# A scan layer and a spectral layer on one core: the scan layer's first and last steps get other banks, another load order and interleaved norm halves

## The chip, the core and the metric

The kernel runs on one core of a Trainium2 chip. A core has five engines with instruction queues of their own: TensorE (PE, matrix products into PSUM), VectorE (DVE), ScalarE (ACT), GpSimd (POOL) and SyncE (SP), which here issues the transfers between the chip's memory and the on-chip memory SBUF. An engine works through its queue in order, and waits on semaphores for the other engines and for transfers. PSUM has eight banks, each of 512 fp32 values on 128 partitions.

The metric is the device time of one execution in microseconds (us), as the median of several runs. Fewer is better.

## The reference

Two layers run one after the other on `x` of shape (4, 128, 128, 128): batch, channels, rows, columns. All is fp32.

```python
# layer 0: a selective scan over the 64 tokens of every 8 x 8 window
tn = layernorm(t) * ln_g + ln_b                 # over the 128 channels
xi, z = split(tn @ W_in + b_in)                 # 256 channels each
xc = silu(causal_conv(xi, conv_w, K=4) + conv_b)
dr, Bm, Cm = split(xc @ W_x)                    # 8, 16 and 16 channels
delta = softplus(dr @ dt_w + dt_b)
h = exp(delta * A) * h + (delta * xc) * Bm      # scan over 64 tokens, 16 states
y = (sum(h * Cm) + xc * D) * silu(z)
x = x + y @ W_out + b_out
# layer 1: norm over channels, 2-D FFT, spectral filters, inverse FFT, MLP, residual
zn = layernorm(x) * gamma + beta
Uf = rfft2(zn) * conj(Phi)                      # 16 filters
S = einsum('bdlxy,lhd->bhxy', irfft2(Uf), Theta)
out = x + W2(gelu(W1(S) + b1)) + b2
```

## The kernel before

Four stages follow each other: `mamba_layer` (layer 0, and the norm of layer 1), `spectra`, `mix` and `images_and_mlp` (the rest of layer 1). Only `mamba_layer` is concerned here.

**Rows and steps.** The image is cut into 64 "rows" (4 images, 16 strips of 8 pixel rows): 1024 tokens of 128 channels each, tile `xt`. A row's scans are cut into 32 units, each of 128 partitions (8 channels x 16 states) and 2x512 tokens. The kernel is written out as one list of slots `s`. Unit `s` is scanned in slot `s` (`scan`, L401): VectorE multiplies the replicated `delta*x` by B (L408) and runs the scan (L410), then POOL multiplies by C (L418). Slots 0 to 2047 hold the scans of all 64 rows.

**What lies around the scans.** Row r's preparation begins some 30 slots before its scans, so from the second row on it stands between the scans of the row before. Row 0's preparation has slots -35 to -6, with no scans beside it. In the same way the last row's output stands, in part, behind the last scan. The order within every engine's queue is the order in which the Python code emits the instructions (`manual_schedule`): in each slot first the `takes`, then fetches, replication, decay, then `make`, `took`, the scan, and `lates`.

The steps of one row's preparation, with their lines: load of `xt` (L173); the norm in two halves of 512 tokens, each of `ln_center` (L150, four matmuls that subtract the mean), `ln_scale` (L157 to L162, ACT: squares with accumulation, Ln, Exp, scaled copies), `ln_back` (L168, four matmuls that turn the tokens back) and `f_affine` (L180, into `tn`); four groups `f_conv` (L202, L200) and four `f_in` (L188), each emptied by ACT (L207, L193); Silu on ACT (L210, L211); for two channel halves the matmuls of `f_dt` (L227) and `f_bc` (L217), ACT's Abs, Relu, Exp and Ln (L237 to L242), and POOL's sum and product (L245, L251), whose results `delta` and `du` SP stores to memory (L254, L257). From there SP fetches them again, replicated over the states, as `dr` (L342, for `exp(delta*A)` at L391) and, for seven of 32 units, `ur` (L352). For the other units TensorE replicates `du` into a bank pair (L376).

The steps behind the scans: `b_gate` (L263), `b_out` and its bias (L272, L274, L280) in two halves into `x1t`, the store of `x1t` (L283), the second norm (same helpers, `b_affine` at L288 into `z`) and the store of `z` (L291). `spectra` loads `z` from memory again (L491).

**PSUM.** The eight banks are given out as: three pairs `du` (the replicated units), one bank `y` (the sums over states) and one bank `one`, which all preparation and output steps share:

```python
        def one(name):
            return ps.tile([P, HB], F32, tag="one", name=name)
```

**Before the first slot** SP loads 17 constants (L61). VectorE and TensorE then fold the causal convolution into the input product (L84 to L106, with matmuls L93 into `one`), and two small weights into one (L108 to L116). `fold` and `fold2` are one after the other in the buffer `ab`. VectorE clears four `dA` tiles and `tn` (L121, L125). Row 0's `xt` is loaded by its `take` in slot -35, which stands behind all of this in SP's queue.

Of the kernel before, what the change touches and what calls it, by code (L numbers as in the profile page):

```python
# [13 lines left out]
F32 = mybir.dt.float32  # L14
BF16 = mybir.dt.bfloat16
AF = mybir.ActivationFunctionType
# [3 lines left out]
P = 128  # L20
# [5 lines left out]
DR = 8  # L26
W = 128
HB = 512
# [5 lines left out]
def mamba_layer(tc, d, x, x1, zb, deltas, dus):  # L34
# [8 lines left out]
    nc = tc.nc  # L43
    B = x.shape[0]
    NH, NW = W // WS, W // WS
    n = WS * W
    U = 32
# [5 lines left out]
    with ExitStack() as ctx:  # L53
# [2 lines left out]
        sb = ctx.enter_context(tc.tile_pool(name="l0_sb", bufs=1))  # L56
        ps = ctx.enter_context(tc.tile_pool(name="l0_ps", bufs=1, space=PSUM))

        def load(name):
            t = cp.tile(list(d[name].shape), F32, tag=name, name=f"c_{name}")  # L60
            nc.sync.dma_start(t, d[name])  # L61
            return t

        def half(t, h):
# [5 lines left out]
        nc.vector.memset(eps, EPS)  # L70
        zeros = cp.tile([P, 2, WS], F32, tag="zeros", name="zeros")
        nc.vector.memset(zeros, 0.0)
        names = "center rsel ssel ln_g ln_b W_in b_in conv_w conv_b W_bc dt_b A_log D W_out b_out gamma beta"
        c = {k: load(k) for k in names.split()}
        A = cp.tile([P, 32], F32, tag="A", name="A")
        nc.scalar.activation(A, c["A_log"], AF.Exp)
        nc.vector.tensor_scalar(A, A, -1.0, None, ALU.mult)
# [6 lines left out]
        fold = sb.tile([P, n], F32, tag="ab", name="fold")  # L84
        nc.sync.dma_start(fold[:, : 2 * P], d["W_in_t"])
# [23 lines left out]
        fold = sb.tile([P, n], F32, tag="ab", name="fold2")  # L109
        nc.sync.dma_start(fold[:DR, : 2 * P], d["W_xdt"])  # L110
        nc.sync.dma_start(fold[:DR, HB : HB + 2 * P], d["dt_w"])
        for ch in range(2):
            t = ps.tile([P, HB], F32, tag="one", name="p_fold")
            w = fold[:DR, ch * P : (ch + 1) * P]
            nc.tensor.matmul(t[:, : 2 * P], w, fold[:DR, HB : HB + 2 * P], start=True, stop=True)
            nc.vector.tensor_copy(W_dt[:, ch], t[:, : 2 * P])  # L116
# [12 lines left out]

        rs = [SimpleNamespace(py={}, yz={}) for _ in rows_all]  # L130
        takes, lates, makes = {}, {}, {}

        def take(slot, f):
            takes.setdefault(slot, []).append(f)
# [8 lines left out]


        def ln_center(o, src, h):
            o.ln = one("ln_cen")
            for q in range(HB // P):
                at = h * HB + q * P
                tokens = getattr(o, src)[:, at : at + P]
                nc.tensor.matmul(o.ln[:, q * P : (q + 1) * P], tokens, c["center"], start=True, stop=True)  # L150

        def ln_scale(o):
            o.cs = sb.tile([P, HB], F32, tag="cs", name="cs", bufs=2)
            r = sb.tile([P, HB // P], F32, tag="ln_r", name="ln_r", bufs=2)
            blocks = [slice(q * P, (q + 1) * P) for q in range(HB // P)]
            for q, k in enumerate(blocks):
                nc.scalar.activation(o.cs[:, k], o.ln[:, k], AF.Square, accum_out=r[:, q : q + 1])  # L157

            nc.scalar.activation(r, r, AF.Ln, bias=eps, scale=1.0 / P)
            nc.scalar.activation(r, r, AF.Exp, scale=-0.5)  # L160
            for q, k in enumerate(blocks):
                nc.scalar.activation(o.cs[:, k], o.ln[:, k], AF.Copy, scale=r[:, q : q + 1])  # L162

        def ln_back(o):
            o.lb = one("ln_back")
            for q in range(HB // P):
                k = slice(q * P, (q + 1) * P)
                nc.tensor.matmul(o.lb[:, k], o.cs[:, k], ident, start=True, stop=True)  # L168


        def f_load(o, b, rows):
            o.xt = sb.tile([P, n], F32, tag="xt", name="xt", bufs=3)
            nc.sync.dma_start(o.xt, x[b, :, rows, :].rearrange("c i w -> c (i w)"))  # L173

        def f_affine(o, h):

# [113 lines left out]
        def b_store_z(o, b, rows):  # L290
            nc.sync.dma_start(zb[b][:, rows, :].rearrange("c i w -> c (i w)"), o.z)  # L291

        def norm(o, src, affine, at):
            for h in range(2):
                made(at + 2 * h, partial(ln_center, o, src, h), partial(ln_scale, o))
                made(at + 2 * h + 1, partial(ln_back, o), partial(affine, o, h))

        for r, (o, (b, rows)) in enumerate(zip(rs, rows_all)):  # L300
            s = U * r - LEAD
            for h in range(2):
                for k in range(2):
                    late(s + LEAD + 16 * h + 8 * k + 11, partial(b_gate, o, h, k))
                made(s + (61, 67)[h], partial(b_out, o, h), partial(b_out_bias, o, h))
            take(s + 72, partial(b_store, o, b, rows))
            norm(o, "x1t", b_affine, s + 89)
            take(s + 96, partial(b_store_z, o, b, rows))
        for r, (o, (b, rows)) in enumerate(zip(rs, rows_all)):
            s = U * r - LEAD  # L310
            take(s - 5, partial(f_load, o, b, rows))
            norm(o, "xt", f_affine, s - 1)
            for i in range(4):
                m, h = divmod(i, 2)
                made(s + (5, 7, 10, 12)[i], partial(f_conv, o, m, h), partial(f_conv_out, o, m, h))
                made(s + (8, 9, 13, 14)[i], partial(f_in, o, 2 + m, h), partial(f_in_z, o, 2 + m, h))
                made(s + (17, 18, 21, 22)[i], partial(f_dt, o, m, h), partial(f_dt_out, o, m, h))
                made(s + (19, 20, 23, 24)[i], partial(f_bc, o, h, m), partial(f_bc_out, o, h, m))
            take(s + 15, partial(f_silu, o))
            for k in range(2):  # L320
                take(s + 19 + 4 * k, partial(f_soft, o, k))
                take(s + 19 + 4 * k, partial(f_delta, o, k))
                take(s + 21 + 4 * k, partial(f_store, o, r, k))
                take(s + 21 + 4 * k, partial(f_du, o, k))
                take(s + 24 + 4 * k, partial(f_store_du, o, r, k))
# [473 lines left out]
```

## Time and profile before

| | us |
|---|---|
| median of 3 runs | 10449.41 |
| lowest and highest | 10445.54, 10451.61 |
| the profiled execution | 10450.79 |
| its span, first to last instruction | 10448.8 |
| first unit's product (L408) begins | 104.69 |
| last scan (L410) ends | 7158.44 |
| `z` of the last row is stored (L291) | 7185.69 |
| first matmul of `spectra` | 7195.28 |

The profile is of one execution, so its times add up to 10448.8 us, not to the median. Of the span, VectorE is busy 86%, TensorE 89%, GpSimd 79%, ScalarE 62%. These are means over stages with different limits. In the scan phase VectorE is busy 936 to 940 of every 1000 us and POOL about 904 to 911 (stretches from 1400 to 2400 and from 3400 to 4400 us). The constants that are loaded first are small: each of the large ones (`rsel`, `W_in`, `W_bc`) has 256 KB and lands 2.6 to 2.9 us after its issue; a row of `x` has 512 KB. TensorE's busy share must be read with care: matmuls are pipelined, and the same matmul takes about twice as long when the granted clock is low.

### The profile page before, as it was taken

Reading aid. Unit: us, or ns where it says so; the run is one execution under the profiler, and the core shown is the slowest. Engines: PE = TensorE matmul, PEld = TensorE weight load, DVE = VectorE, ACT = ScalarE, POOL = GpSimd, SP = SyncE. Lnnn points to the kernel's source line nnn. Section 1 sums busy time; section 2 is a strip of 40 time slices with the busy share of each in tenths; the row PEclk is TensorE's granted clock in tenths of the full one; section 3 lists DMA queues with packets and bytes.
Section 4 is the critical chain, followed back from the end, with each engine's and each line's share of the span. In section 5 each row is a group of like instructions: output and inputs, shape, how many; then the busy total and the mean of one; then the engine's idle time right before and its main releaser. Section 6 shows DMA issues by size and latency. Waiting matters only on the chain.

```text
span 10448.8 us, 143616 instructions
## 1 busy us (share of the span) xinstructions
PE 9293.9 (89%) x48900; PEld 5027.3 (48%) x48900; DVE 8980.1 (86%) x7234; ACT 6524.3 (62%) x12463; POOL 8231.4 (79%) x4188
## 2 busy tenths in 40 slices
PE   6888888888888888888888888887889999998999
PEld 2333333333333333333333333335889999998766
DVE  5999999999999999999999999995389999998433
ACT  5776777777777777777777677773344444444433
POOL 5899998998998998989989899893079999997000
PEclk8999989989999999999999999997999999999999
DMA  4777677777776776777767767775521111112332
GB/s 150 213 229 220 213 223 218 217 219 219 225 221 213 226 222 214 223 217 225 221 210 228 218 215 223 219 221 160 148 68 34 35 35 36 36 36 62 136 128 93
DMA packets 1168110, 1794.06 MB, mean 172 GB/s; under 512 B 368641, under 2 KB 436497, under 8 KB 1166225
## 3 DMA queue, kind: packets, MB, share of 16 engines
q1 hardware_dynamic: 1167376, 1784.88, 56.6%
q8 instruction: 387, 6.34, 0.3%
q14 instruction: 347, 2.83, 0.1%
HBM read 1481.44 MB, written 303.04 MB: 171 GB/s over the span
## 4 chain that ended last, share of the span: by engine, by line
PE 58%; ACT 20%; DVE 9%; DMA 7%; issue 4%; POOL 1%; SPq 1%; DVEq 0%; ACTq 0%; POOLq 0%
PE p_v L578 13%; DVE hs L410 6%; PE p_du L376 6%; PE p_conv L202 5%; DMA dr<-delta 5%; ACT part L589 5%; PE p_bc L217 5%; PE p_dt L227 4%; PE p_y L428 4%; DVE p_du L408 3%; PE p_out L274 2%; ACT dA L391 2%; PE ln_cen L150 2%; ACT p_du L391 2%; PE p_h L672 2%
## 5 line engine op out<-in xcount | busy, mean ns | idle before, releaser
L418 POOL TENSOR_TENSOR hs<-hs,bc 128x1024 f32<-128x1024 f32 x2048 | 4806.3, 2372 | 408.9 <-DVE hs L410 357.3
L410 DVE TENSOR_TENSOR_SCAN hs<-dA,p_du 128x1024 f32<-128x1024 f32 x1600 | 3659.0, 2287 | 208.2 <-DVE p_du L408 4.9
L591 POOL TENSOR_TENSOR acc<-acc,part 128x512 f32<-128x512 f32 x1430 | 1829.3, 1319 | 640.6 <-ACT part L589 640.6
L408 DVE TENSOR_TENSOR p_du<-p_du,bc 128x1024 f32<-128x1024 f32 x1600 | 1935.8, 1210 | 219.6 <-PE p_du L376 215.0
L391 ACT ACTIVATE dA<-dr,A 128x504 f32<-128x504 f32 x3200 | 2072.0, 704 | 33.1 <-DVE hs L410 23.7
L578 PE MATMUL p_v<-theta,xk 128*128 128x128 f32 x16640 | 1941.4, 277 | 87.9 <-ACT part L589 51.9
L578 PEld LDWEIGHTS p_v<-theta,xk 128*128 128x128 f32 x16640 | 1883.1, 192 | 146.2 <-ACT part L589 118.9
L595 DVE SCALAR_TENSOR_TENSOR acc<-p_v,phi,acc 128x512 f32<-128x512 f32 x2470 | 1672.4, 740 | 114.2 <-PE p_v L578 87.5
L376 PE MATMUL p_du<-du,c_rsel 32*128 32x512 f32 x6400 | 1364.3, 678 | 370.2 <-DVE hs L410 370.2
L589 ACT ACTIVATE part<-p_v,phi 128x512 f32<-128x512 f32 x1430 | 904.8, 686 | 803.9 <-PE p_v L578 800.3
L428 PE MATMUL p_y<-hs,c_ssel 128*32 128x512 f32 x8192 | 1225.7, 634 | 134.2 <-DVE yz L263 82.9
L410 DVE TENSOR_TENSOR_SCAN hs<-p_du,ur 128x1024 f32<-128x1024 f32 x448 | 1019.0, 2275 | 86.8 <-ACT p_du L391 60.5
L356 POOL TENSOR_TENSOR ur<-ur,bc 128x1024 f32<-128x1024 f32 x448 | 1063.1, 2373 | 10.7 <-DMA ur<-du 10.7
L202 PE MATMUL p_conv<-tn,W_conv 128*128 128x512 f32 x2048 | 1007.3, 616 | 3.2 <-ACT xc L207 1.6
L376 PEld LDWEIGHTS p_du<-du,c_rsel 32*128 32x128 f32 x6400 | 370.4, 192 | 1081.1 <-issue 780.6
L227 PE MATMUL p_dt<-xc,W_dt 128*128 128x512 f32 x1024 | 619.8, 736 | 48.0 <-ACT dl L238 42.3
L391 ACT ACTIVATE p_du<-dr,A 128x504 f32<-128x504 f32 x896 | 613.9, 685 | 29.1
L428 PEld LDWEIGHTS p_y<-hs,c_ssel 128*32 128x32 f32 x8192 | 184.3, 111 | 887.5 <-issue 571.2
L207 ACT ACTIVATE xc<-p_conv,b_conv 128x512 f32<-128x512 f32 x256 | 176.2, 688 | 639.3 <-PE p_conv L202 639.3
L245 POOL TENSOR_TENSOR dl<-dl,ab 128x1024 f32<-128x1024 f32 x128 | 302.6, 2364 | 338.5 <-ACT ab L242 338.5
L202 PEld LDWEIGHTS p_conv<-tn,W_conv 128*128 128x128 f32 x2048 | 346.8, 189 | 455.2 <-issue 247.9
L168 PE MATMUL ln_back<-ident,cs 128*128 128x128 f32 x2048 | 339.5, 316 | 222.3 <-ACT cs L162 216.6
(100 smaller groups left out, 10341.0 us busy)
## 6 DMA issues: line engine op xcount, KB each, us to landing
dr<-delta SPq DMA_DIRECT2D x4096, 256.0 KB, 5.2
ur<-du SPq DMA_DIRECT2D x896, 256.0 KB, 6.4
delta<-dl SPq DMA_DIRECT2D x128, 512.0 KB, 2.9
du<-du SPq DMA_DIRECT2D x128, 512.0 KB, 5.4
xf<-x SPq DMA_DIRECT2D x8, 4160.0 KB, 16.4
xk<-xf SPq DMA_DIRECT2D x130, 256.0 KB, 3.8
sf<-acc SPq DMA_DIRECT2D x520, 64.0 KB, 1.7
s<-sf SPq DMA_DIRECT2D x8, 4160.0 KB, 13.4
```

The source lines that it names most:

```text
L202: nc.tensor.matmul(windows(o.pc), W_conv[:, ch, k], moved, start=(k == 0), stop=(k == K - 1))
L356: nc.gpsimd.tensor_tensor(fetched[s], fetched[s], both(o.bc[0], h), ALU.mult)
L376: nc.tensor.matmul(u.bank[:, j % 2], c["rsel"][p, u.i], half(u.o.du[p, u.ch], u.h), start=True, stop=True)
L391: nc.scalar.activation(u.dA[:, q, :, 1:], u.delta[:, q].rearrange("p (w t) -> p w t", t=L)[:, :, 1:], AF.Exp, scale=A[:, g : g + 1],)
L408: nc.vector.tensor_tensor(u.bu, u.bu, both(u.o.bc[0], u.h), ALU.mult)
L410: nc.vector.tensor_tensor_scan(u.hs.rearrange("p q t -> p (q t)"), u.dA.rearrange("p q w t -> p (q w t)"), u.bu.rearrange("p q t -> p (q t)"),
L418: nc.gpsimd.tensor_tensor(u.hs, u.hs, both(u.o.bc[1], u.h), ALU.mult)
L428: nc.tensor.matmul(o.py[h, ch][32 * j : 32 * j + 32], c["ssel"][:, u.i], units[s + j // 2].hs[:, j % 2], start=(u.i == 0), stop=False, ski ...
L578: nc.tensor.matmul(t[:, b], o.xk[:, b, r], theta[:, k], start=True, stop=True)
L589: nc.scalar.activation(part, v[of], AF.Copy, scale=factor)
L591: nc.gpsimd.tensor_tensor(apart, apart, part, ALU.add)
L595: nc.vector.scalar_tensor_tensor(mine, v[of], factor, mine, ALU.mult, ALU.add)
```

## The change

Six edits, all in `mamba_layer`:

1. ACT's table set with Ln, Exp and others is loaded first of all, by name.
2. Row 0's tokens are loaded first on SP's queue, ahead of the constants. ACT issues four transfers itself: `W_in_t`, `conv_w`, `b_in`, `conv_b`. The other constants come in another order.
3. `fold2` gets a buffer of its own (one of the two `z` buffers), so its two loads need not wait for `fold`.
4. The fold matmuls, and every step that calls `one` in a slot before -1 or from 2048 on, use the three bank pairs `du` in turn (the first bank of a pair) instead of the bank `one`. At that time the units don't use them.
5. Row 0's first norm and the last row's second norm emit center, center, back, back instead of center, back, center, back. The last row's norm follows its output directly, and its `z` store stands right behind its `x1t` store. The other rows keep their order.
6. The `dA` tiles and `tn` are cleared by POOL instead of VectorE.

```diff
+        nc.scalar.preload_act_table_set("natural_log_exp_and_others")
+
         def load(name):
             t = cp.tile(list(d[name].shape), F32, tag=name, name=f"c_{name}")
-            nc.sync.dma_start(t, d[name])
+            (nc.scalar if name in "conv_w b_in conv_b" else nc.sync).dma_start(t, d[name])
+            return t
+
+        def load_tokens(b, rows):
+            t = sb.tile([P, n], F32, tag="xt", name="xt", bufs=3)
+            nc.sync.dma_start(t, x[b, :, rows, :].rearrange("c i w -> c (i w)"))
             return t
...
-        names = "center rsel ssel ln_g ln_b W_in b_in conv_w conv_b W_bc dt_b A_log D W_out b_out gamma beta"
+
+        fold = sb.tile([P, n], F32, tag="ab", name="fold")
+        fold2 = sb.tile([P, n], F32, tag="z", name="fold2", bufs=2)
+        nc.scalar.dma_start(fold[:, : 2 * P], d["W_in_t"])
+        first = load_tokens(*rows_all[0])
+        names = "center ln_g ln_b conv_w b_in conv_b W_in D A_log dt_b W_bc rsel ssel W_out b_out gamma beta"
         c = {k: load(k) for k in names.split()}
+        nc.sync.dma_start(fold2[:DR, : 2 * P], d["W_xdt"])
+        nc.sync.dma_start(fold2[:DR, HB : HB + 2 * P], d["dt_w"])
...
-            t = ps.tile([P, HB], F32, tag="one", name="p_fold")
+            t = ps.tile([P, 2, HB], F32, tag="du", name="p_du", bufs=3)[:, 0]
...
-            nc.vector.memset(t, 0.0)
+            nc.gpsimd.memset(t, 0.0)
             dAs.append(t)
...
-        nc.vector.memset(tn, 0.0)
+        nc.gpsimd.memset(tn, 0.0)

         def one(name):
+
+            if one.free:
+                return ps.tile([P, 2, HB], F32, tag="du", name="p_du", bufs=3)[:, 0]
             return ps.tile([P, HB], F32, tag="one", name=name)
...
-        def norm(o, src, affine, at):
+        def norm(o, src, affine, *slots):
             for h in range(2):
-                made(at + 2 * h, partial(ln_center, o, src, h), partial(ln_scale, o))
-                made(at + 2 * h + 1, partial(ln_back, o), partial(affine, o, h))
+                made(slots[h], partial(ln_center, o, src, h), partial(ln_scale, o, h))
+                made(slots[2 + h], partial(ln_back, o, h), partial(affine, o, h))
...
+            last = r == R - 1
             take(s + 72, partial(b_store, o, b, rows))
-            norm(o, "x1t", b_affine, s + 89)
-            take(s + 96, partial(b_store_z, o, b, rows))
+            norm(o, "x1t", b_affine, *((s + k) for k in ((68, 69, 70, 71) if last else (89, 91, 90, 92))))
+            take(s + (72 if last else 96), partial(b_store_z, o, b, rows))
...
-            take(s - 5, partial(f_load, o, b, rows))
-            norm(o, "xt", f_affine, s - 1)
+            if r == 0:
+                o.xt = first
+            else:
+                take(s - 5, partial(f_load, o, b, rows))
+            norm(o, "xt", f_affine, *((s + k) for k in ((-1, 0, 1, 2) if r == 0 else (-1, 1, 0, 2))))
...
         for s in range(-LEAD - 5, U * R + 99 - LEAD):
+            one.free = not -1 <= s < U * R
```

`ln_center`, `ln_scale` and `ln_back` take the half `h` as well and keep `o.ln[h]` and `o.cs[h]` apart, so that both halves can be under way; `cs` had two buffers already.

More of the change, by code (lines that the diff above doesn't have):

```diff
@@ L83, in mamba_layer @@
         early = cp.tile([P, 2, WS, K - 1], F32, tag="early", name="early")
-        fold = sb.tile([P, n], F32, tag="ab", name="fold")
-        nc.sync.dma_start(fold[:, : 2 * P], d["W_in_t"])
         for ch in range(2):
             nc.vector.tensor_scalar(skip[:, ch], ident, c["D"][:, ch : ch + 1], None, ALU.mult)
-            t = ps.tile([P, HB], F32, tag="one", name="p_fold")
+            t = ps.tile([P, 2, HB], F32, tag="du", name="p_du", bufs=3)[:, 0]
             for k in range(K):
@@ L108, in mamba_layer @@
         W_dt = cp.tile([P, 2, 2 * P], F32, tag="W_dt", name="W_dt")
-        fold = sb.tile([P, n], F32, tag="ab", name="fold2")
-        nc.sync.dma_start(fold[:DR, : 2 * P], d["W_xdt"])
-        nc.sync.dma_start(fold[:DR, HB : HB + 2 * P], d["dt_w"])
         for ch in range(2):
-            t = ps.tile([P, HB], F32, tag="one", name="p_fold")
-            w = fold[:DR, ch * P : (ch + 1) * P]
-            nc.tensor.matmul(t[:, : 2 * P], w, fold[:DR, HB : HB + 2 * P], start=True, stop=True)
+            t = ps.tile([P, 2, HB], F32, tag="du", name="p_du", bufs=3)[:, 0]
+            w = fold2[:DR, ch * P : (ch + 1) * P]
+            nc.tensor.matmul(t[:, : 2 * P], w, fold2[:DR, HB : HB + 2 * P], start=True, stop=True)
             nc.vector.tensor_copy(W_dt[:, ch], t[:, : 2 * P])
@@ L120, in mamba_layer @@
             t = cp.tile([P, 2, WS, L], F32, tag=f"dA{i}", name="dA")
-            nc.vector.memset(t, 0.0)
+            nc.gpsimd.memset(t, 0.0)
             dAs.append(t)
         tn = cp.tile([P, NW, K - 1 + L], F32, tag="tn", name="tn")
-        nc.vector.memset(tn, 0.0)
+        nc.gpsimd.memset(tn, 0.0)
         def one(name):
+            if one.free:
+                return ps.tile([P, 2, HB], F32, tag="du", name="p_du", bufs=3)[:, 0]
             return ps.tile([P, HB], F32, tag="one", name=name)
-        rs = [SimpleNamespace(py={}, yz={}) for _ in rows_all]
+        rs = [SimpleNamespace(py={}, yz={}, ln={}, cs={}) for _ in rows_all]
         takes, lates, makes = {}, {}, {}
@@ L145, in ln_center @@
         def ln_center(o, src, h):
-            o.ln = one("ln_cen")
+            o.ln[h] = one("ln_cen")
             for q in range(HB // P):
@@ L149, in ln_center, with ln_scale @@
                 tokens = getattr(o, src)[:, at : at + P]
-                nc.tensor.matmul(o.ln[:, q * P : (q + 1) * P], tokens, c["center"], start=True, stop=True)
-        def ln_scale(o):
-            o.cs = sb.tile([P, HB], F32, tag="cs", name="cs", bufs=2)
+                nc.tensor.matmul(o.ln[h][:, q * P : (q + 1) * P], tokens, c["center"], start=True, stop=True)
+        def ln_scale(o, h):
+            cs = o.cs[h] = sb.tile([P, HB], F32, tag="cs", name="cs", bufs=2)
             r = sb.tile([P, HB // P], F32, tag="ln_r", name="ln_r", bufs=2)
@@ L156, in ln_scale @@
             for q, k in enumerate(blocks):
-                nc.scalar.activation(o.cs[:, k], o.ln[:, k], AF.Square, accum_out=r[:, q : q + 1])
+                nc.scalar.activation(cs[:, k], o.ln[h][:, k], AF.Square, accum_out=r[:, q : q + 1])
             nc.scalar.activation(r, r, AF.Ln, bias=eps, scale=1.0 / P)
@@ L161, in ln_scale, with ln_back @@
             for q, k in enumerate(blocks):
-                nc.scalar.activation(o.cs[:, k], o.ln[:, k], AF.Copy, scale=r[:, q : q + 1])
-        def ln_back(o):
+                nc.scalar.activation(cs[:, k], o.ln[h][:, k], AF.Copy, scale=r[:, q : q + 1])
+        def ln_back(o, h):
             o.lb = one("ln_back")
@@ L167, in ln_back @@
                 k = slice(q * P, (q + 1) * P)
-                nc.tensor.matmul(o.lb[:, k], o.cs[:, k], ident, start=True, stop=True)
+                nc.tensor.matmul(o.lb[:, k], o.cs[h][:, k], ident, start=True, stop=True)
         def f_load(o, b, rows):
-            o.xt = sb.tile([P, n], F32, tag="xt", name="xt", bufs=3)
-            nc.sync.dma_start(o.xt, x[b, :, rows, :].rearrange("c i w -> c (i w)"))
+            o.xt = load_tokens(b, rows)
         def f_affine(o, h):
```

## The prediction

> **What bounds the kernel now.** I read the page's 40 slices first, then the busy time by stretch, the timeline of both ends, the queue waits of SP, and last the chain of waits around the places found.
>
> ```profile
> DVE  5999999999999999999999999995389999998433
> PEclk8999989989999999999999999997999999999999
> ```
>
> The slices show one VectorE-bound scan phase (slices 2 to 27) with a hole at its start and another at its end. The change touches only these. The stretches size the first hole; columns are stretch and length, then busy us (instructions) of PE, PEld, DVE, ACT, POOL, then clock, DMA share, GB/s:
>
> ```profile
> 25.40:46.60 21.20, 8.25 (x32) 7.10 (x32) 4.60 (x5) 12.32 (x34) 0.00 (x0) 1.00 0.00 0
> 46.60:75.20 28.60, 22.42 (x48) 8.79 (x48) 0.00 (x0) 5.50 (x8) 0.00 (x0) 1.00 0.00 1
> 75.20:103.30 28.10, 17.32 (x32) 5.92 (x32) 0.00 (x0) 17.10 (x20) 7.03 (x3) 0.94 0.17 56
> 103.30:137.50 34.20, 20.11 (x84) 10.07 (x84) 25.13 (x14) 22.26 (x56) 23.49 (x11) 0.70 0.94 281
> ```
>
> Until 103.3 us no engine is full: PE and ACT alternate. The timeline (start, length, instruction, in brackets the idle time before it) says why:
>
> ```profile
> 24.90 0.42 DVE L116 COPY W_dt<-p_fold 128x256 f32<-128x256 f32 x1 [1.31 <-PE p_fold L115]
> 25.38 2.08 PE L150 MATMUL ln_cen<-c_center,xt 128*128 128x128 f32 x8 [0.52 <-DVE W_dt L116]
> 28.66 1.28 ACT L159 ACT_TABLE_LOAD   x1
> 30.27 1.28 ACT L160 ACT_TABLE_LOAD   x1
> 36.03 2.07 PE L150 MATMUL ln_cen<-c_center,xt 128*128 128x128 f32 x8 [0.90 <-ACT tn L180]
> 53.53 1.13 PE L202 MATMUL p_conv<-tn,W_conv 128*128 128x512 f32 x2 [0.78 <-ACT xc L207]
> 100.92 2.35 POOL L245 TENSOR_TENSOR dl<-dl,ab 128x1024 f32<-128x1024 f32 x1 [7.29 <-ACT ab L242]
> 103.30 0.34 SPq L254 DMA_DIRECT2D delta<-dl  x1
> ```
>
> Each matmul group starts as soon as ACT or DVE has emptied the single bank `one`: 25.38, 36.03 and 53.53 all wait for a reader. At 103.30 SP stores the second delta half; the fetches of the next steps' `dr` stand behind that store, so scans can't run on before it. The tail, same columns:
>
> ```profile
> 7170.64 1.16 PE L150 MATMUL ln_cen<-c_center,x1t 128*128 128x128 f32 x8 [0.78 <-ACT x1t L280]
> 7176.89 0.78 ACT L288 ACTIVATE z<-ln_back,c_beta,c_gamma 128x512 f32<-128x512 f32 x1 [2.17 <-PE ln_back L168]
> 7177.72 2.08 PE L150 MATMUL ln_cen<-c_center,x1t 128*128 128x128 f32 x8 [0.87 <-ACT z L288]
> 7184.89 0.78 ACT L288 ACTIVATE z<-ln_back,c_beta,c_gamma 128x512 f32<-128x512 f32 x1 [2.16 <-PE ln_back L168]
> 7185.69 0.32 SPq L291 DMA_DIRECT2D z<-z  x1
> ```
>
> The last norm does one half, then the other; in the chain of waits the next stage's first load (7188.71) waits for the `z` store of 7185.69.
>
> **What the Trainium skill says.** "ScalarE: Activation LUTs", section "What ACT_TABLE_LOAD costs": a load is about 1.28 us plus 1.38 us of drain. The trace agrees on the load, but Ln begins 1.29 us after its load began, so I price 1.3 us each. "TensorE: Matmul & The Clock Gate", "Part 1: The HAM clock gate": the array runs at half rate until a window of some 3.4 us was busy, and falls back after an idle one, the window running free. The trace shows both rates (the same four center matmuls in 2.08 and 1.16 us) and a warm-up after about 4.3 us at 46.61; but at 7158.77 it stayed slow for over 5 us. I carry both values. "DMA: Bandwidth & Descriptors", "Issuing engines are not separate DMA queues": starting transfers from a second engine saves only issue time. Before, ACT starts none, so the trace can't say.
>
> **Part by part.** The built instruction order of both kernels differs only ahead of the first scans and after row 63's first `b_out`; all between, queues included, has the same order. The span is 10448.8 us, the execution 10450.8, the median shown 10449.4: a saving is taken off the last unchanged.
>
> (a) Start to the end of the first center matmuls, 27.46 us before. SP now issues x (512 KB), center, ln_g, ln_b. W_in is the ninth transfer and waits for x to land, since eight semaphores are used in turn. x alone took 3.5 us in the trace, other rows' x 7.4 (median), 9.1 at most. With center and W_in_t beside it I take 4.5: W_in at 5.2, D 5.7, A_log 6.2, landing 2.24 later (8.15 less 5.91 before) at 8.4. Before, ACT had it at 8.15: 0.3 lost. But W_in_t, first matmul operand at 11.22 before, now goes first from ACT; four ACT issues at SP's 0.48 each, even behind the 1.28 table load, end by 4 us. So DVE's diagonals set the start: first at 9.1, first fold matmul 9.5 instead of 11.22 (-1.7). DVE's order is unchanged, hence the second fold group ends at 16.2 (17.91 before). W_xdt and dt_w no longer wait for buffer `ab` (SP waited for L106 until 20.02); they land by about 13.5, under the fold. W_dt's two matmuls follow at 16.3 to 18.7 (1.2 each), and x is there: center runs 18.8 to 19.9 warm or 20.8 cold. I take 20.4: **-7.1**. DVE's five memsets (4.6 us) go to POOL, idle from 1.3 to 88.9; ident's 128x128 memset there took 0.20, so 8 times the size is some 1.6 each, at the other end the 2.35 of a tensor op: done by 9 to 13, needed at about 26. Without cover it would cost at most those 13 us.
>
> (b) To the first conv matmul, 19.15 us before (27.46 to 46.61). After: with three banks both centers run at once; ACT does 2.9 us a half (118.30 to 121.17 for row 1: squares 1.16, Ln 0.33, Exp 0.24, scale 1.14) without four table loads, 5.2 us; the back matmuls of half 0 lie beside half 1's squares. 5.8 for both halves, then two affines of 0.8: 7.4, or 7.95 with cold back matmuls. I take 7.6: **-11.5**. The added preload hides under the waiting for A_log.
>
> (c) Conv and in, 28.6 us before: eight groups, each 3.96 or 1.14 of PE plus 0.77 of ACT and handover, the first conv cold (6.15). After, PE runs through with ACT behind it: 4x3.96 + 4x1.14 + 0.75 = 21.2 warm, 23.4 cold at first. I take 22.6: **-6.0**.
>
> (d) To the end of delta's second half on POOL, 28.07 before. Table load and Silu 3.2 stay. Then PE cold 3.65, and five groups of 1.98 in a row (dt, bc, bc, dt, dt) end at 13.6; the last dt pair of ACT and Exp/Ln take 3.4, POOL 2.35: 3.2 + 19.35 = 22.6: **-5.5**. ACT's copies of `bc` are the next late item, done 1.2 us ahead of POOL.
>
> (e) From there SP's order is unchanged. Step 0 moves up 2 us more, but step 3's `dr`, issued at 108.06 and 108.84, lands by 117.7 at a 94% DMA share: everything counted from the delta store repeats. Worth 0; channel 0's du store now ends nearer to it, at most 5.5 us given back. Scans are VectorE-bound, so the shift passes to their end.
>
> (f) Tail. `x1t` is complete at 7170.59. Both centers, then 1.2 + 5.8 + two affines 1.5: 7179.2 warm, 7179.8 cold, instead of 7185.67: **-6.2**. The x store (7170.61) lands in 6.1 to 8.5 us, ahead of the z store. Row 63's second `b_out` no longer waits for `one`, worth 0: PE is still at p_y (7166.16) when that bank is free (7164.98).
>
> Sum: -7.1 - 11.5 - 6.0 - 5.5 - 6.2 = -36.3; 10450.8 gives 10414.5, the median 10413.1. I say 10413. Unknown costs: all warm -39; x landing after 7.4, PE cold throughout -30.
>
> **Rivals.** B, the start gives part back: x takes 9.1 (+4.6), PE stays cold (+1.5), the first fetches collide (+5.5): 10425. For it: 281 GB/s at 103 to 137; against: x alone took 3.5. C, scans can't start earlier because DMA, not the delta store, sets them; then only the tail counts: 10443. Against: SP waited for POOL until 103.30, and DMA share was 0.17 ahead of it. D, slower: with another starting phase the long scan settles in a worse rhythm. Its place is rows 1 to 63; its price is visible as 553 to 556 VectorE instructions per 1000 us. The slowest stretch against the mean 554.5 is 0.27%, 19 us in 7000; it decides from 0.52%, 36 us. At 0.8%, 56 us: 10469. Against: six stretches agree and the order is the same. E, the flag leaves the old bank in use: excluded, the built prologue writes `p_du` banks.
>
> **Chances.** A as worked 0.81, own range 10406 to 10421; B 0.11; C 0.04; D 0.04. What a measurement can tell is about 0.2%, 21 us, so faster means under 10428.5: A and most of B, 0.89; C and the rest of B, 0.07 no change; D 0.04 slower. Range 10405 to 10428: A with the 3 us by which runs differ, and B.
>
> **What would show it.** Right: first center end near 20, first conv near 28, one table load ahead of Silu, delta's second store near 73, the z store 9 us after `x1t` instead of 15. Wrong: gaps on PE between conv groups, POOL memsets late for `tn`, a first delta store earlier but scans not, or fewer than 553 VectorE instructions per 1000 us.

## The result, and the profile after

The changed kernel takes 10404.0 us (median of five runs, 10398.08 to 10406.42), the kernel before 10445.97 beside it (five runs, 10436.68 to 10451.61): -42.0 us, ratio 0.9959 [0.9945, 0.9974]. Forecast was 10413.0, at least 10405. The profiled execution of after has a span of 10396.1 us, so it is the lowest of its five runs; before's was 10448.8. Of these 52.7 us some ten lie in the scan phase. Below it turns out that two executions of one kernel differ there by as much.

The 40 slices of after:

```profile
DVE  6999999999999999999999999995389999998433
...
PEclk8999999999999999999999999998999999999999
```

The picture of before, with a shorter hole in slice 1. The stretches of after show what became of it (stretch and length; busy us and instructions of PE, PEld, DVE, ACT, POOL; clock, DMA share, GB/s). They are the norm, the convolution and input products, the delta steps, and the first 34.2 us of the scans:

```profile
17.78:27.08 9.30, 6.27 (x34) 5.65 (x33) 0.78 (x4) 6.85 (x30) 0.00 (x0) 1.00 0.00 0
27.08:46.10 19.02, 18.30 (x48) 8.30 (x48) 0.00 (x0) 5.49 (x8) 0.00 (x0) 1.00 0.00 1
46.10:67.49 21.39, 17.80 (x44) 7.49 (x44) 1.23 (x1) 17.63 (x22) 7.05 (x3) 0.92 0.20 74
67.49:101.69 34.20, 18.28 (x70) 9.38 (x71) 23.06 (x13) 20.82 (x55) 23.50 (x11) 0.65 0.95 278
```

The 48 matmul records of the second stretch now fill it (18.30 of 19.02 us; 22.42 of 28.60 before). The fourth is much like before's from 103.30 on: VectorE is busy 23.06 of the 34.20 us after the second `delta` store (25.13 before), at a DMA share of 0.95 (0.94). The timeline of after (start, length, instruction, idle time before it):

```profile
0.73 1.28 ACT L59 ACT_TABLE_LOAD   x1 [0.73 <-PEq L804]
0.74 0.39 SPq L68 DMA_DIRECT2D xt<-in_x_dram  x1
...
1.25 3.62 POOL L130 MEMSET dA<- 128x1024 f32 x4
...
4.83 0.33 SPq L63 DMA_DIRECT2D c_W_in<-in_W_in_dram  x1
...
9.20 2.08 PE L105 MATMUL p_du<-fold 128*128 128x128 f32 x8 [9.20 <-DVE fold L103]
...
17.78 3.78 PE L162 MATMUL p_du<-c_center,xt 128*128 128x128 f32 x16
...
27.08 1.10 PE L213 MATMUL p_du<-tn,W_conv 128*128 128x512 f32 x2 [0.99 <-ACT tn L191]
...
31.01 0.69 ACT L218 ACTIVATE xc<-p_du,b_conv 128x512 f32<-128x512 f32 x1 [4.08 <-PE p_du L213]
...
34.67 0.69 ACT L218 ACTIVATE xc<-p_du,b_conv 128x512 f32<-128x512 f32 x1 [2.97 <-PE p_du L213]
...
35.53 0.69 ACT L204 ACTIVATE zs<-p_du,c_b_in 128x512 f32<-128x512 f32 x1 [0.17 <-PE p_du L199]
...
36.39 0.69 ACT L204 ACTIVATE zs<-p_du,c_b_in 128x512 f32<-128x512 f32 x1 [0.17 <-PE p_du L199]
...
46.13 1.28 ACT L221 ACT_TABLE_LOAD   x1
...
49.38 5.40 PE L238 MATMUL p_du<-xc,W_dt 128*128 128x512 f32 x8 [4.00 <-ACT xc L221]
...
58.05 3.60 PE L238 MATMUL p_du<-xc,W_dt 128*128 128x512 f32 x8
...
60.59 0.69 ACT L248 ACTIVATE ab<-p_du,c_dt_b 128x512 f32<-128x512 f32 x1 [1.51 <-POOL dl L256]
...
61.48 3.60 PE L228 MATMUL p_du<-xc,c_W_bc 128*128 128x512 f32 x8
...
61.74 0.69 ACT L248 ACTIVATE ab<-p_du,c_dt_b 128x512 f32<-128x512 f32 x1
...
67.49 0.33 SPq L265 DMA_DIRECT2D delta<-dl  x1
```

The eight center matmuls (16 records) stand in one line; the wait for the reader between the halves is gone. ACT's readers of the convolution are 3.66 us apart (31.01, 34.67), those of the input product 0.86 (35.53, 36.39), and each waits for PE: PE never waits for them. At 60.59 is a wait that the prediction did not have: ACT's first `ab` of the second channel half waits for POOL's sum of the first, since `ab` has one buffer. It cost little: the second group of that `dt` pair was through PE only near 61.48, where the next group begins, and ACT took it at 61.74. The tail of after, same columns:

```profile
7124.70 2.05 PE L162 MATMUL p_du<-c_center,x1t 128*128 128x128 f32 x16 [0.78 <-ACT x1t L291]
...
7128.06 1.26 PE L180 MATMUL p_du<-ident,cs 128*128 128x128 f32 x8 [1.31 <-ACT cs L174]
...
7130.83 1.26 PE L180 MATMUL p_du<-ident,cs 128*128 128x128 f32 x8 [1.51 <-ACT cs L174]
...
7131.43 1.48 ACT L299 ACTIVATE z<-p_du,c_beta,c_gamma 128x512 f32<-128x512 f32 x2
7132.94 0.32 SPq L302 DMA_DIRECT2D z<-z  x1
```

From the end of `x1t` to the `z` store it is 8.3 us instead of 15.1.

By the prediction's terms, in us. A second execution of after (called f2 below) stands beside it, since TensorE's clock met it differently. Its first conv pair took 2.04 us, and 1.10 in the profiled execution; below, such stretches are called cold and warm:

| term | before | after | gain | f2 | gain | predicted |
|---|---|---|---|---|---|---|
| (a) start to the first square on ACT | 27.49 | 19.89 | 7.6 | 19.64 | 7.9 | 7.1 |
| (b) to the first conv matmul | 19.12 | 7.19 | 11.9 | 8.00 | 11.1 | 11.5 |
| (c) to Silu's table load | 28.60 | 19.05 | 9.6 | 22.14 | 6.5 | 6.0 |
| (d) to the second `delta` store | 28.09 | 21.36 | 6.7 | 21.36 | 6.7 | 5.5 |
| (f) `x1t` to the `z` store | 15.10 | 8.29 | 6.8 | 9.09 | 6.0 | 6.2 |
| sum | | | 42.6 | | 38.2 | 36.3 |

### The profile page after: what moved, and what is told of

It is laid out like the page before. It is cut to its first block, busy times and chain, and to the rows that moved or that the text cites. A ratio compares the mean times of both kernels' runs of the same rounds, so it can differ in the third digit from the quotient of the medians.

```text
span 10396.1 us, 143613 instructions
## 1 busy us (share of the span) xinstructions
PE 9268.0 (89%) x48900; PEld 5013.8 (48%) x48900; DVE 8974.8 (86%) x7229; ACT 6518.1 (63%) x12459; POOL 8235.2 (79%) x4193
## 4 chain that ended last, share of the span: by engine, by line
PE 59%; ACT 19%; DVE 9%; DMA 6%; issue 3%; POOL 1%; SPq 1%; DVEq 0%; ACTq 0%; POOLq 0%
PE p_v L594 13%; DVE hs L425 6%; PE p_du L391 6%; PE p_conv L213 6%; ACT part L605 5%; PE p_dt L238 5%; DMA dr<-delta 5%; PE p_bc L228 5%; PE p_y L443 4%; DVE p_du L423 3%; PE p_out L285 2%; ACT dA L406 2%; ACT p_du L406 2%; PE ln_cen L162 2%; PE p_h L688 2%
## 5 line engine op out<-in xcount | busy, mean ns | idle before, releaser
L371 POOL TENSOR_TENSOR ur<-ur,bc 128x1024 f32<-128x1024 f32 x448 | 1062.3, 2371 | 10.6 <-DMA ur<-du 10.6
L228 PE MATMUL p_bc<-xc,c_W_bc 128*128 128x512 f32 x1008 | 493.4, 612 | 36.0 <-ACT dl L249 36.0
```

## The experiments

Theory T1: the gain is the sum of these stages, and the scans repeat. Theory T2: the scan phase itself runs in another rhythm when it starts at another time (the prediction's rival D, with either sign). The profiled pair speaks for T2: from the second `delta` store to the end of the last scan it is 7055.1 us before and 7045.0 after. "Stage" below is always a stretch of the table, from the profile of the kernel named. Times are compared within a group of kernels that ran on one chip; the medians of before differ between groups, from 10437 to 10466.

**First group: parts of the change.** Before: 10448.56 us.

e1: the load order, the table load by name, the buffer of `fold2` and POOL's clearing alone; one bank, and norms in turn.

```diff
...
-            t = ps.tile([P, 2, HB], F32, tag="du", name="p_du", bufs=3)[:, 0]
+            t = ps.tile([P, HB], F32, tag="one", name="p_fold")
...
-            norm(o, "x1t", b_affine, *((s + k) for k in ((68, 69, 70, 71) if last else (89, 91, 90, 92))))
-            take(s + (72 if last else 96), partial(b_store_z, o, b, rows))
+            norm(o, "x1t", b_affine, *((s + k) for k in (89, 91, 90, 92)))
+            take(s + 96, partial(b_store_z, o, b, rows))
...
-            norm(o, "xt", f_affine, *((s + k) for k in ((-1, 0, 1, 2) if r == 0 else (-1, 1, 0, 2))))
+            norm(o, "xt", f_affine, *((s + k) for k in (-1, 1, 0, 2)))
...
-            one.free = not -1 <= s < U * R
+            one.free = False
```

> Edits 1, 2, 3 and 6 alone (table set, loads, fold2's buffer, memsets); every step keeps the bank one and norms go half by half. T1 (the gain is the sum of the start's and the tail's terms; what I under-sized is the conv and in term): first center matmuls end near 22 us, first conv near 36, delta's second store near 93 instead of 103.3, tail 15.1 us as before; total about 10.6 us under before. T2 (part of the measured gain comes from a better rhythm of the scan phase once it starts at another time): the stretch from delta's second store to the last scan's end is some 10 us shorter than the 7055 of before, as in the changed kernel (7045), so about 20 us under before.

10434.58 us, 0.9987 [0.9981, 0.9994]. The second `delta` store is at 93.11 instead of 103.30: 10.2 us of stages, of which 5.4 come to the first square and 5.0 from the norm. The median gives 14.0. The scan stretch is 7051.9 (7055.1 before; T2 has some 7045).

e2: the kernel before with edit 4 alone.

```diff
...
-            t = ps.tile([P, HB], F32, tag="one", name="p_fold")
+            t = ps.tile([P, 2, HB], F32, tag="du", name="p_du", bufs=3)[:, 0]
...
         def one(name):
+            if one.free:
+                return ps.tile([P, 2, HB], F32, tag="du", name="p_du", bufs=3)[:, 0]
             return ps.tile([P, HB], F32, tag="one", name=name)
...
+            one.free = not -1 <= s < U * R
```

> The three banks in turn alone, on the kernel before (old loads, norms half by half). T1: the conv and in stage (first conv to the last zs) takes about 19 to 21 us instead of 28.6, the stage from there to delta's second store about 21.4 instead of 28.1; with 1 us at W_dt, 2.5 in the norm and 2.5 in the tail that is 21 us under before. If instead the conv and in term was right as predicted (22.6), the stage shows 22 to 23 us and the total is 18 under before. T2: 10 us more than either, in the scan phase.

10427.44 us, 0.9977 [0.9969, 0.9986], -21.1. The store is at 85.78. (c) gives 6.7, with a slow first group, and (d) 6.7: in these two terms the banks alone give what after shows in such an execution (6.5 and 6.7 in f2). The first square comes 1.1 earlier, the norm gives 2.9 and the tail 3.5, 21.0 in all.

e3: after, with one bank and norms in turn for the last row.

```diff
-            last = r == R - 1
+            last = False
...
-            one.free = not -1 <= s < U * R
+            one.free = s < -1
```

> The changed kernel with the tail of before (bank one, norm half by half, late z store). T1: the start as in the changed kernel (delta's second store at 67.5), the tail from x1t's end to the z store 15.1 us instead of 8.3; 6.8 us over the changed kernel, 35 under before. T2: the scan phase as in the changed kernel, near 7045 us; T1 leaves it anywhere in the band in which runs of before differ (15 us).

10409.39 us, 0.9963 [0.9951, 0.9976]. The stage from `x1t` to the `z` store is 15.09 again; all of (f) is this edit.

e4: after, with convolution and input product in one bank again.

```diff
-            one.free = not -1 <= s < U * R
+            one.free = s < -LEAD + 5 or -LEAD + 16 < s < -1 or s >= U * R
```

> The changed kernel with only row 0's conv and in steps back in the bank one. T1: this stage alone goes back from 19.0 us to 26.4 (TensorE warm at its start) or 28.6 (cold), all other stages keep their lengths: 7.4 to 9.6 us over the changed kernel. If the term was 6.0 as I predicted and the rest came from elsewhere, the rise is 6 or less.

10408.34 us, 0.9963 [0.9950, 0.9975]. The stage (c) is as long as before: 28.96 us (28.60 before, 19.05 or 22.14 after). The timeline of e4 shows the handover of the one bank, conv and input product:

```profile
34.72 1.13 PE L213 MATMUL p_conv<-tn,W_conv 128*128 128x512 f32 x2 [0.78 <-ACT xc L218]
...
38.68 0.69 ACT L218 ACTIVATE xc<-p_conv,b_conv 128x512 f32<-128x512 f32 x1 [4.02 <-PE p_conv L213]
...
39.42 1.13 PE L199 MATMUL p_in<-tn,c_W_in 128*128 128x512 f32 x2 [0.78 <-ACT xc L218]
```

A group starts 4.70 us after the one before it (34.72 to 39.42), of which 3.96 pass until ACT can start. In after, with banks to spare, readers are 3.66 us apart. So a handover costs 1.04: the 0.74 from ACT's start to the next group, and the 0.30 by which start to reader is longer than the distance of readers in a row. The times don't show this: the medians of e3 and e4 lie 39.2 and 40.2 us under before, where their stages (start and tail) give 32.5 and 32.3. That e4 loses the conv term is shown by its stage alone.

**Second group: the norm, the table load, and what is left.** Before: 10437.28 us.

e5: after, row 0's norm in turn.

```diff
-            norm(o, "xt", f_affine, *((s + k) for k in ((-1, 0, 1, 2) if r == 0 else (-1, 1, 0, 2))))
+            norm(o, "xt", f_affine, *((s + k) for k in (-1, 1, 0, 2)))
```

> The changed kernel with row 0's first norm half by half again (center, back, center, back), everything else kept. T1 (the gain is the sum of the stages): the norm stage, first squares to first conv, takes 11.0 us (16.2 of the kernel with only the banks, less four table loads of 1.3) instead of 7.2 to 8.0; the rest of the start and the tail as in the changed kernel; 3 to 4 us over it. T2 (the scan phase has a better rhythm): the stretch from delta's second store to the last scan's end stays near 7045 whatever the start does.

10396.97 us, 0.9967 [0.9954, 0.9979]. The norm takes 11.23 us instead of 7.2 or 8.0. After itself did not run in this group, so the expected 3 to 4 us show in the stage only.

e6: after without the table load by name.

```diff
-        nc.scalar.preload_act_table_set("natural_log_exp_and_others")
```

> The changed kernel without the table set named at the start. T1: four table loads come back inside the norm, two in each half, 1.3 us each: the norm stage takes 12.4 to 13.2 us, total 5.2 us over the changed kernel. If a drain came with each load, 2.66 us each, it is 10.6 us. Were the loads hidden beside TensorE's work, nothing changes.

10400.23 us, 0.9966 [0.9954, 0.9978]. The norm takes 13.11 us, with four loads in it; the timeline of e6 shows those of the first half:

```profile
21.25 1.28 ACT L169 ACT_TABLE_LOAD   x1
...
22.86 1.28 ACT L170 ACT_TABLE_LOAD   x1
```

Against 7.2 and 8.0 a load costs 1.3 to 1.5 us; a drain behind each (2.66 us a load, from the figures that the prediction quotes) would have made it 10.6 for the four, and is not seen. Of the 11.1 to 11.9 us of (b), naming the table set is thus the largest part (5.1 to 5.9), and the order of the halves gives 3.2 to 4.0; the banks alone gave 2.9 in e2.

e7: what is left at the start. The folds move behind the norm in the queues: ACT and PE do the norm as soon as `x` is there.

```diff
...
+        early_steps = ((1, partial(fold_conv, 0)), (3, partial(fold_conv, 1)), (3, decay_scale), (15, fold_dt))
...
+            for at, f in early_steps:
+                if s == at - LEAD:
+                    f()
```

> A further step: the fold of the convolution weights is emitted between the steps of row 0's norm, ahead of its first conv, and the small W_dt fold behind the conv and in steps, so that the center matmuls start when x lands. T1 (the start is one chain whose length passes to the end): center at about 5 us instead of 17.8, squares from 7, first conv at 15 to 16 instead of 27.1, set by the second half's folded weights; 11 us under the changed kernel. Rival: the start is no longer the chain but something beside it, such as the delta stores and dr transfers at a 94% DMA share; then delta's second store moves up by 11 us and the last scan's end by clearly less.

10383.2 us, 0.9950 [0.9937, 0.9962]. The timeline of e7:

```profile
5.66 3.75 PE L165 MATMUL p_du<-c_center,xt 128*128 128x128 f32 x16 [5.66 <-DMA c_center<-in_center_dram]
...
9.20 1.91 PE L108 MATMUL p_du<-fold 128*128 128x128 f32 x8
...
14.92 1.10 PE L216 MATMUL p_du<-tn,W_conv 128*128 128x512 f32 x2
```

Fold matmuls fill PE's waits in the norm; the second `delta` store is at 56.13, 11.4 us ahead of after's, and the last scan ends 14.2 ahead of it (7098.26, 7112.50), the rest within the scatter of the scan stretch. The rival, that the end moves by clearly less, fell.

e8: e7, and in row 0 all `dt` products ahead of the `bc` products, with a second buffer for `ab`.

```diff
...
-                made(s + (17, 18, 21, 22)[i], partial(f_dt, o, m, h), partial(f_dt_out, o, m, h))
-                made(s + (19, 20, 23, 24)[i], partial(f_bc, o, h, m), partial(f_bc_out, o, h, m))
+                made(s + ((17, 18, 20, 21) if r == 0 else (17, 18, 21, 22))[i], partial(f_dt, o, m, h), partial(f_dt_out, o, m, h))
+                made(s + ((23, 24, 25, 26) if r == 0 else (19, 20, 23, 24))[i], partial(f_bc, o, h, m), partial(f_bc_out, o, h, m))
...
```

> As the kernel with the norm first, and in row 0 the dt matmuls of both channel halves stand ahead of the bc ones, with a buffer of its own for the second half's softplus. T1: ACT no longer waits for POOL's first sum (60.59 in the changed kernel), delta's second store comes 2 to 4 us earlier relative to Silu; 13 to 15 us under the changed kernel. Rival: POOL's order sum, product, sum holds the second sum back, and only 0 to 1 us more than the kernel with the norm first is won.

10378.32 us, 0.9946 [0.9933, 0.9958]. The store moves by 1.9 us, to 54.22, a little short of the 2 to 4 expected. The first scan begins at 58.34, later than in e7 (57.51); in both it waits for ACT's `dA`, which waits for the fetched `dr`, so the earlier `delta` store did not move it. The median is 4.9 lower than e7's; of this, 3.6 us are a shorter scan stretch in the profiled execution (7038.5 against 7042.1), no more than the scatter that the fourth group shows.

**Third group: start time against rhythm.** Before: 10466.05 us. e9 and e10 are before and after unchanged.

> The kernel before, once more, for a profile beside those of this call. T1 (the gain is the sum of the stages of the start and of the tail, 42.6 us in the two traces): the same stages as in the first profile within 1 us, and the stretch from delta's second store to the last scan's end within 5 us of the other kernels of this call. T2 (a better rhythm of the scan phase with the changed start): this stretch is some 10 us longer than in the changed kernel.

10464.35 us, 1.0000 [0.9991, 1.0008].

> The changed kernel, once more, on the same chip as the kernel before. T1: 40 to 43 us under it, by whether TensorE starts the first conv warm or cold; scan stretch as in the kernel before within 5 us. T2: scan stretch 10 us shorter.

10417.7 us, 0.9956 [0.9943, 0.9968]: 48.4 under before, where T1 had 40 to 43. Second `delta` stores at 104.03 and 71.78; scan stretches 7070.9 and 7060.9. Again 10 us shorter, as T2 has it.

e11: after, with 34 clearings of an unused tile on VectorE ahead of the folds, so that its scans start as late as before's.

```diff
+        idle = sb.tile([P, 2, HB], F32, tag="hs", name="idle", bufs=6)
+        for _ in range(34):
+            nc.vector.memset(idle, 0.0)
```

> The changed kernel with 34 more memsets on VectorE ahead of the fold, some 36 us, so that its scans begin when those of the kernel before begin. T1: the delay passes to the end in full, 35 to 37 us over the changed kernel, and the scan stretch stays as it is. T2: the scan stretch goes back to that of the kernel before, so that it comes 45 us over the changed kernel.

10454.89 us, 0.9991 [0.9982, 0.9999]. That is 37.2 over e10 (T1: 35 to 37, T2: 45). The store is at 102.83, the scan stretch 7062.4, that of e10 and not of e9. Both speak against T2 in the form that the starting time sets the rhythm. The stretch of one execution can't decide it, as the fourth group shows; the median of 13 is the better evidence.

e12: e8 with four matmuls that nobody reads, put where TensorE waits for Silu.

```diff
...
+        def keep_warm():
+            t = ps.tile([P, 2, HB], F32, tag="du", name="p_warm", bufs=3)[:, 0]
+            for _ in range(4):
+                nc.tensor.matmul(t, ident, c["W_in"], start=True, stop=True)
...
```

> As the kernel with dt first, and four matmuls whose result nobody reads stand between W_dt's fold and row 0's first dt matmul, to keep TensorE's clock up while ACT computes Silu. T1: the first dt pair takes 2.0 us instead of 3.65, delta's second store comes 1.5 us earlier, 1 to 2 us under the kernel with dt first. If ACT's second Silu and table load end later than the matmuls, nothing is won.

10402.48 us, 0.9940 [0.9928, 0.9952]: 15.2 less than e10. Against its before it has the lowest ratio of all, but its interval overlaps with e8's, which ran in another group: the gain over e8 is shown by the stages only. The timeline of e8, and then that of e12, at the `dt` products:

```profile
37.04 10.06 PE L241 MATMUL p_du<-xc,W_dt 128*128 128x512 f32 x16 [2.94 <-ACT xc L224]
```

```profile
34.02 3.70 PE L465 MATMUL p_warm<-c_W_in,ident 128*128 128x512 f32 x8
...
37.56 7.03 PE L241 MATMUL p_du<-xc,W_dt 128*128 128x512 f32 x16
```

The same products take 7.03 instead of 10.06 us, and Silu to the second `delta` store 16.7 instead of 19.1 us; 1.5 us were expected.

**Fourth group: chance or kernel.** What remained was the 10 us of the scan stretch, seen in two pairs. Four single executions, two of each kernel in turn, on one chip; nothing is edited.

> The kernel before, unchanged, to see how much of the scan stretch (second delta store to the end of the last scan) belongs to the kernel and how much to the execution. Both theories: the start and the tail as in its two earlier profiles, second delta store at 103 to 104 us, last x1t to z store 15.1. Theory 'kernel' (something in the old code makes the scans 10 us longer): this stretch is 8 to 12 us longer than those of both executions of the changed kernel beside it. Theory 'execution' (which TensorE clock row 0 and row 1 meet is chance, and so is what the later rows make of it): the two executions of one kernel differ by 4 us or more, and the two kernels' values overlap or lie under 4 us apart.

> The changed kernel, unchanged. Both theories: second delta store at 67 to 72 us, x1t to z store 8.3 to 9.1. Theory 'kernel': the scan stretch is 8 to 12 us shorter than in both executions of the kernel before, and the first row of scans is 108.2 us long. Theory 'execution': the stretch can be as long as one of the kernel before, and the first row can be 111 us long as well, where row 1's convolution meets a slow TensorE.

> The kernel before once more, on the same chip. Theory 'kernel': scan stretch within 2 us of the execution ahead. Theory 'execution': 4 us or more away from it, or no farther from the changed kernel's than from that.

> The changed kernel once more. Theory 'kernel': scan stretch within 2 us of its execution ahead, 8 to 12 us under the kernel before. Theory 'execution': 4 us or more away from it, or overlapping with the kernel before.

| | f1, before | f2, after | f3, before | f4, after |
|---|---|---|---|---|
| time | 10445.98 | 10398.82 | 10434.28 | 10404.68 |
| second `delta` store | 104.24 | 71.14 | 103.83 | 71.11 |
| from there to the last scan's end | 7046.3 | 7039.9 | 7038.3 | 7049.5 |

Before differs from itself by 8.0 us and after by 9.6, and the two overlap: the 10 us don't belong to the kernel. A rest of a few us can't be excluded with four executions. Part of the difference can be seen in row 1's convolution, which stands among the first scans. In f1 it ran slow and VectorE's product stood 3.38 us for PE; in f3 it ran fast and no such wait is there. The timeline of f1, then of f3:

```profile
141.32 4.69 PE L202 MATMUL p_conv<-tn,W_conv 128*128 128x512 f32 x6
...
148.11 1.23 DVE L408 TENSOR_TENSOR p_du<-p_du,bc 128x1024 f32<-128x1024 f32 x1 [3.38 <-PE p_du L376]
```

```profile
137.03 2.82 PE L202 MATMUL p_conv<-tn,W_conv 128*128 128x512 f32 x6
```

Against f1 and f3 beside them, the stages (a) to (f) of f2 and f4 add up to 39.0 and 39.5 (38.2 and 39.0 against the first profile); the means of the two pairs of times lie 38.4 apart.

**What the scatter goes with.** The record has the mean granted TensorE clock of every execution, and the times follow it. Of the 82 executions of before outside the first comparison, the 16 at a clock of 0.936 have a median of 10466.8 us, the 15 at 0.941 one of 10450.9, the five at 0.946 one of 10437.2: some 3 us for each thousandth. The groups of before differ mainly by this, and the chip alone does not set it: e9 and f1 ran on the same one. The scan stretch follows it too: before has 7070.9 (e9, 0.936), 7055.1 (first profile, 0.941), 7046.3 (f1, 0.944) and 7038.3 (f3, 0.946); after has 7060.9 (e10, 0.937), 7049.5 (f4) and 7045.0 (first profile, both 0.943) and 7039.9 (f2, 0.945). Part of the difference shows as waiting: VectorE's product (L408) waited 226.9 us for TensorE's replication in e9 and 207.4 in f3, as their pages have it:

```profile
L408 DVE TENSOR_TENSOR p_du<-p_du,bc 128x1024 f32<-128x1024 f32 x1600 | 1935.0, 1209 | 231.8 <-PE p_du L376 226.9
```

```profile
L408 DVE TENSOR_TENSOR p_du<-p_du,bc 128x1024 f32<-128x1024 f32 x1600 | 1935.6, 1210 | 212.4 <-PE p_du L376 207.4
```

No run sets the clock, so that it is the cause is not shown. Still it makes kernels comparable. At 0.942 the median of before is 10446.99 (4 executions) and that of after 10404.23 (3), 42.8 apart; at 0.943 10446.31 (7) and 10404.00 (3), 42.3 apart; single executions of after at 0.937 and 0.945 give 45 and 41. So compared, e3 is 7.3 over after (10411.50, three executions at 0.942), close to the 6.8 of its tail. But e4 is only 3.9 over it (10407.87, four at 0.943) with a stage that is 6.8 to 9.9 longer; that is not explained.

## Why the prediction was right and where it was wrong

**Right: the place, the mechanism and the split.** Each stage shortened for the reason given, and e1 to e6 took the reasons away in turn. **Wrong: the size.** The step that failed is the length of a matmul group that runs through, in (c) and again in (d). The prediction took 3.96, 1.14 and 1.98 us a group, and the runs show 3.66, 0.86 and 1.72. The saving was thus worked too small: 36.3 us, where the stages give 38 to 43.

Rival B (the start gives part back) fell. `x` did hold up W_in, as worked: eight transfers went out, and the ninth stood 2.3 us for `x`, but only until 4.83 (5.2 was taken). Rival C fell, as the first scan follows the store (68.89 behind 67.49; before 106.02 behind 103.30). Rival D, slower scans, fell with the result. Scans at 0 in (e) agree with e11 and f1 to f4 within the scatter of 8 to 10 us from execution to execution.

**(a) 7.6 for 7.1.** The first fold matmul is at 9.20 (9.5), and center follows at 17.78 (18.8). The folds between cost less than assumed, 8.6 instead of 9.3 us. POOL's five clearings were done by 5.8 us (four in 3.62 from 1.25 on, then `tn`), not by 9 to 13.

**(b) 11.9 or 11.1 for 11.5.** The 7.4 (warm) and 7.95 (cold) of the text are 7.19 and 8.00 in the traces.

**(c) 9.6 or 6.5 for 6.0: the step that failed.** The sum "4x3.96 + 4x1.14 + 0.75 = 21.2 warm, 23.4 cold" charged the groups with the lengths that they have after a wait; run through, a group is 3.66 and 0.86 (the distances of ACT's readers). That is 4x0.30 + 4x0.28 = 2.3 less, and 19.05 was measured warm. Cold it is 22.14. The first two groups of f2 in its timeline:

```profile
27.64 2.04 PE L213 MATMUL p_du<-tn,W_conv 128*128 128x512 f32 x2 [0.99 <-ACT tn L191]
...
34.66 0.69 ACT L218 ACTIVATE xc<-p_du,b_conv 128x512 f32<-128x512 f32 x1 [7.17 <-PE p_du L213]
...
38.32 0.69 ACT L218 ACTIVATE xc<-p_du,b_conv 128x512 f32<-128x512 f32 x1 [2.97 <-PE p_du L213]
```

The first reader waits 7.02 us (27.64 to 34.66) instead of 3.93, so a cold start adds 3.1, where the prediction added 2.2. That the chosen 22.6 is near the measured cold 22.14 is thus partly luck: groups too long and a cold start too short nearly cancel. Most executions of this stage ran cold (f2, f4, e3, e5 and e10); in the profiled one, which ran warm, the error stands bare. Since the warm value was 2.3 too high, "all warm -39" was no bound: the stages gave 42.6.

**(d) 6.7 for 5.5.** "Then PE cold 3.65, and five groups of 1.98 in a row" is the same error: run through, pairs of groups begin 3.43 us apart (54.62, 58.05, 61.48), so a group takes 1.72. PE was done after 12.1 us (49.38 to 61.48) instead of 13.6. ACT began 0.26 later (61.74), which the sum had at nothing; 0.20 of it is ACT's usual distance behind PE (54.62 to 54.82 in the same trace), so the unforeseen wait for `ab` cost next to nothing. ACT's 3.4 and POOL's 2.4 are as worked.

**(f) 6.8 or 6.0 for 6.2.** As worked.

**The range** took 3 us for the difference of runs, from three runs within 6 us. Five of before lay within 15, and the median to which the sum was applied was 10449.41, that beside the result 10445.97: 3.4 of the 9.0 us by which the forecast was missed are in the starting value, 5.6 in the difference. The three comparisons of the unchanged kernels gave 42.0, 48.4 (third group) and 38.4 (fourth); the interval of the first, 27 to 57 us, holds the predicted 36.3. At equal clock the two kernels lie some 42 us apart, so most of the 5.6 is no scatter of the clock. The mis-sized terms account for 6.3 us in the warm profile and for some 3 in f2 and f4 beside their befores; what makes the rest in cold executions is open.

## What to carry to other kernels

Where several steps share one PSUM bank and the kernel has idle banks in that phase, count the handovers, 1.04 us each here, and price groups in a row by the distance of their readers in a stretch without waits, not by the time from start to reader of one that began after a wait. A change of some tens of us in 10 ms is judged by its stages, and whether a stretch that the change leaves alone has really changed by a second execution of each kernel. Executions are compared at equal granted clock, where the record has it. What the start still holds is found by asking which engine waits for nothing but the order in its queue: doing the norm ahead of the folds moved the second `delta` store another 11 us ahead, and filling the wait for Silu with four unread matmuls 2.5 us of the stage behind it.

## What was not expected of the hardware

The same program meets two TensorE rates in the same place: after's first conv pair took 1.10 us in one execution and 2.04 in another, so the stage 19.05 or 22.14. In e8 an idle stretch of 2.94 us ahead of the `dt` products was enough for them to begin slow: their weight loads stand 0.85 us apart up to 42.33 and 0.43 from 43.08 on, so that 16 records took 10.06 us against 7.03. Before's executions spread over 44 us with the mean granted clock, from 10429.39 us at 0.947 to 10473.34 at 0.935. A table load on ACT did not hold up ACT's own transfers: the load ran from 0.73 to 2.01, and its issues stand at 0.76, 1.18, 1.66 and 2.14. POOL clears a 128x1024 fp32 tile in 0.9 us, as fast as VectorE (0.91 in e11).
